# One tap of the first half of the channels of a depthwise convolution: 64-row matmuls in two of four residues replaced by an addition on VectorE, with the residues and the parts of an iteration in another order

## The chip, the cores and the metric

The kernel runs on 1 core of one Trainium2 chip. The metric is the device time of one launch in microseconds (us). Before the change it is 1837.94 us, the median of 3 runs (1837.26 to 1841.47).

## What is computed

Input x has the shape (4, 128, 96, 96). It is normalised by groups of channels, and then a small state-space layer runs over the image four times: along rows, along rows backwards, along columns, along columns backwards. The four results are mixed by a 1x1 convolution (`fuse_w`) and added to x. One direction is:

```
t = grouped1x1(x, in_proj_w)               # 512 channels: 256 of u, 256 of gate
u = conv5(silu(u))                         # depthwise, 5 taps along the sequence
s = ssm_in(u);  a = 0.999 + 0.0009 * sigmoid(ssm_delta(u))
b, c = tanh(ssm_b(u)), tanh(ssm_c(u))
h = scan(h * a + b * s)                    # written with cumulated logarithms
u = u + ssm_out(c * h + d * s)
y = out_proj(mix(u * sigmoid(gate)))
```

All is float32. The first 128 channels of u and the other 128 take different ways in the kernel, called j = 0 and j = 1 below.

## The kernel before, in words

**Units.** A batch has two phases, order V (columns) and H (rows), and each of them works on the forward and the backward direction at once, called s = 0 and s = 1. A phase has NS = 6 steps of 16 lines. Positions of a line are taken modulo R = 4, and one iteration `t` does one such *residue* p of one step: 384 positions (N) of both directions. So there are 4 x 2 x 6 x 4 = 192 iterations; `k = t % 4` is the place in the step, and in the kernel before k is also p. In the second half of a phase the two directions meet the lines that the other one has had, so that the activations `sil` and the gates are not computed again but read back, mirrored, from copies in DRAM (`kept`, `kept_sil`; `fresh(step)` and `mirror(n)` say which).

**The convolution.** Five taps. For j = 1 the taps are ScalarE's first (L718) and four multiply-adds on VectorE (L720, the last one into `u`), in PSUM banks 0 and 1. For j = 0 `sil` keeps the four residues in the four groups of 32 partitions, so that one matmul sums over residues: `conv` has 8 matmuls of 128 rows by 32 columns (weights `band`) over one of two neighbouring columns, and the rest of the taps lie in the other column: `less_both` has 8 matmuls of 64 rows by 32 columns (weights `less`). `less_rows` picks the 64 rows. For residues 1 and 2 two of the residues in those rows have a tap; for residues 0 and 3 only one tap lies there, so that half of these 64 rows meet weights of zero. PSUM is then copied to `u` by L1063. The trace has two records, called passes here, for each matmul in the program.

**One iteration** (`pair_of_tiles`, t >= 8; `pair` does the first eight). It works on the convolution of iteration t, and on the gating and output of iteration n = t - 6 (LAG), whose units are `bi` and `bi + 1`. In TensorE's order the parts are called as follows.

- *W*: `accumulate`, twice 8 matmuls of 128 rows with `w_fin` for iteration n - 1. ScalarE copies the product to `ys` (L825, L827), and GpSimd adds it to `acc` (L844).
- *conv* and *less*: as above, into banks `cb`.
- *block*: 32 matmuls of 32 by 32, in which four row groups work at a time: 16 tiles of input projection (`in_proj_tile`, for the step ahead) or gate (`gate_tile`), called `tile_x` after the change, and 16 tiles of `out_tile` (ssm_out of bi), which add to banks 0 to 3. Two loops, j = 1 and j = 0. Input and gate tiles go to banks `cb` and `db`.
- *proj*: 16 matmuls of 128 rows of iteration t (`w_proj`, operand `main` in the profile), into `db`. ScalarE makes `tm` (L757), copies half of `tb` (L758) and takes the tanh of the other half (L763); GpSimd makes the decay and the product (L765, L766).

Around it: `under(bi, s)` (L553) copies u of n into banks 2s and 2s + 1, so that out_tile adds to it. Bank 0 and 1 are also those of the taps: `under(bi, 0)` can only follow the last tap of iteration t, and the next first tap only the gating of bi. `gating` (L659) is VectorE's, two an iteration. `scale_s` (L775) is a ScalarE multiply. The activations of the block are silu (L491, L500) or tanh (L557, L563). `scan` (L792) runs in k < 2 for the step before; `outputs` (L798 to L801) is GpSimd's. `stats_chunks` (L405) takes statistics of the next batch, `stats_finish` hands out its end in small pieces at k > 1.

**Order of the work.** It is written by hand: the code's order is each engine's order. All loads and stores (`load_front` L280, `load_gate` L295, `load_chunks` L401, `load_kept` L598 and L600, `keep_silu` L468, `load_silu` L475, `send` L807, the reload L1018, the kept gates L1095) are issued by SyncE (SP in the profile), in order, each one waiting for what it needs before the next can leave.

Of the kernel before, what the change touches and what calls it, by code (L numbers as in the profile page):

```python
# [47 lines left out]
P = 128  # L48
# [8 lines left out]
R = 4  # L57
# [5 lines left out]
UB = 8  # L63
NP = NS * R


@with_exitstack
def conv_preact_kernel(
# [28 lines left out]
    for ph, (b, order, dirs) in enumerate(phases):  # L97
        for st in range(NS):
            for p in range(R):
                for s in range(2):  # L100
                    units.append(
                        {
                            "b": b,
                            "order": order,
                            "lay": dirs[s][0],
                            "dir": dirs[s][1],
                            "st": st,
                            "step": ph * NS + st,
                            "p": p,
                            "s": s,  # L110
                            "k": 2 * p + s,
                            "id": f"{ph}_{st}_{p}_{s}",
                        }
                    )
# [172 lines left out]
    def mirror(n):  # L287

        return None if n % NP < NP // 2 else NP - 1 - n % NP

# [42 lines left out]
    b_in, w_tap, b_proj = w_small[:, 64:72], w_small[:, 72:77], w_small[:, 77:79]  # L333
    d_sb, b_mix, b_out, b_fuse = (w_small[:, a:b] for a, b in ((79, 80), (80, 82), (82, 83), (83, 84)))
    w_out = w_out_fuse[:, 0:HID]
    w_fuse = w_out_fuse[:, HID : HID + 4 * P].rearrange("p (d c) -> p d c", d=4)
# [18 lines left out]
    id32 = wp.tile([P, 32], F32, name="id32")  # L355
    ident = wp.tile([P, P], F32, name="ident")
    make_identity(nc, ident)
# [3 lines left out]
    for s in range(2):  # L361
# [21 lines left out]
    kept = [  # L383
        [dp.tile([P, 2, 2, N], F32, tag=f"kept{e}_{m}", name=f"kept{e}_{m}") for m in range(NP // 2 - 2)]
        for e in range(2)
# [4 lines left out]
    def chunks_of(t):  # L390

        un = units[2 * t]
        b, k = un["b"] + 1, t % R
        if un["order"] == "V" and b < B and k > 1:
            return [(b, un["st"] * R + 2 * (k - 2) + e) for e in range(2)]
        return []

    def load_chunks(t):
        for b, c in chunks_of(t):
            chunks[b, c] = wk.tile([P, SC], F32, tag="xs", bufs=4, name=f"xs_{b}_{c}")  # L400
            nc.sync.dma_start(chunks[b, c], xr[b, :, bass.ts(c, SC)])  # L401
# [169 lines left out]
    def sigmoids(bi, to):  # L571
        bn = stats[units[bi]["b"]][1]
        n = bi // 2
        gv = gates[n % 2]
        for s in range(2):

            for j in (1, 0) if s and to == GATE[False] else (0, 1):
                nc.scalar.activation(
                    gv[:, s, j, :],
                    bank(to[2 * s + j])[:, :N],  # L580
                    AF.Tanh,
                    bias=bn[:, 2 + j : 3 + j],
                    scale=0.5,
                )
            load_gate(bi + s + UB)
        if n % NP < NP // 2 - 2:
            nc.sync.dma_start(kept[n // NP % 2][n % NP], gv)

    old_gates = {}

    def tile_of(n):
        m = mirror(n)
        return gates[((n % NP if m is None else m) + n // NP) % 2]

    def load_kept(n):
        m = mirror(n)
        if n % NP < 3 and NP <= n < NU // 2:
            nc.sync.dma_start(tile_of(n), kept[n // NP % 2][n % NP])  # L598
        if n < NU // 2 - R and m is not None and m < NP // 2 - 2:
            nc.sync.dma_start(tile_of(n), kept[n // NP % 2][m])  # L600
# [70 lines left out]

    def conv(i, banks):

        step, p = units[i]["step"], units[i]["p"]
        sil, k, b0 = blocks(step), less_of(p), min(banks)
        for s in range(2):
            for g in range(4):
                mm(bank(b0 + s), g, band[:, s, p, g, :], columns(step, sil[s][:, g, :], 1 - k),
                   True, False)

# [131 lines left out]
    def accumulate(bu, bk, adder=nc.gpsimd, last=False):  # L812
# [9 lines left out]
        if not direct:  # L822
            ys = wk.tile([P, N], F32, tag="ys", bufs=4, name=f"ys_{bu['id']}")
            if s == 0 and bu["order"] == "H":
                nc.scalar.activation(ys, y, AF.Identity, bias=b_fin)  # L825
            else:
                nc.scalar.copy(ys, y)  # L827
            y = ys
# [11 lines left out]
        def add():  # L840
            if direct and s == 0:
                adder.scalar_tensor_tensor(part, y, b_fin, part, ALU.add, ALU.add)
            else:
                adder.tensor_add(part, y, part)  # L844
            if bu["order"] == "H" and bu["st"] >= NS // 2 and bu["p"] == R - 1:

                done.extend((b, bass.ts(2 * st + e, LN * WW // 2)) for e in range(2))
# [147 lines left out]
    def pair_of_tiles(t):  # L995
        i, k, n, end = 2 * t, t % R, t - LAG, NU // 2
        bi, last = 2 * n, t == end - 1
        cb, db = ((4, 5), (6, 7))[:: 1 if t % 2 == 0 else -1]
        late = (n - 1) % (NP * 2) == 0
        step, g = divmod(t + R, R)  # L1000
        fronted, gated = fresh(step), None
# [9 lines left out]
        for e in soon:  # L1011
            load_kept(e)
        soon.clear()
        if t < end - 2:
            send()
        if len(reload) == 4 and (k == 1 or late):
            for b, r in reload:
                nc.sync.dma_start(accf[:, r], xr[b, :, r])  # L1018
            reload.clear()
        if t == LAG + 2:  # L1020
            for j in (1, 0):
# [6 lines left out]
            for s in range(2):  # L1028
                load_gate(bi + s + UB)
        new_u(i)  # L1030
        taps(i, (1, 2))
        piece = later and k > 1
        if piece:
            free[0] = SSM + 2
            next(later[0], None)
        taps(i, (3, 4))
        if piece:
            next(later[0], None)
# [9 lines left out]
        held.clear()  # L1048
        adds = [accumulate(waiting.pop(0), b, *((nc.vector, True) if last else ())) for b in db]
        if late:  # L1050
            held.extend(adds)
        else:
            for add in adds:
                add()

        conv(i, cb)
        under(bi, 0)
        less_both(i, cb)
        if k == 1:
            outputs(i - 10)  # L1060
        stats_chunks(t)
        for s, copy in enumerate((nc.scalar.copy, nc.scalar.copy if k < 2 else nc.vector.tensor_copy)):
            copy(us[i][:, s, 0, :], bank(cb[s])[:, :N])  # L1063
# [12 lines left out]

        if fronted:
            for s in range(2):
                silu(step, g, s, 1, db[s])
        elif gated is not None:  # L1080
            for s in range(2):
                tanh_one(gated, to, s, 1, db[s])
        gating(bi, 0)
        first_tap(i + 2)
# [7 lines left out]
        elif gated is not None:  # L1092
            tanh_both(gated, to, 0, cb[0])
            if gated % NP < NP // 2 - 2:
                nc.sync.dma_start(kept[gated // NP % 2][gated % NP], to)  # L1095
# [5 lines left out]
        un = units[i]  # L1101
        if un["order"] == "V" and un["b"] + 1 < B and un["st"] == NS - 1 and k == R - 1:
# [20 lines left out]
    def tail():  # L1123
# [66 lines left out]
        for i, s, e in ((-2, 1, 0), (-1, 0, 0), (-1, 0, 1), (-2, 1, 1), (-1, 1, 0), (-1, 1, 1)):  # L1190
# [17 lines left out]
            else:  # L1208
                nc.vector.scalar_tensor_tensor(part, y, b_fin, part, ALU.add, ALU.add)
            if bu["p"] == R - 1:  # L1210
                region = bass.ds(lines * WW, LN // 2 * WW)
                nc.sync.dma_start(out[bu["b"], :, region], accf[:, region])

    def start():
# [42 lines left out]
        def burst(j, g):  # L1257
            for s in range(2):
                in_proj(0, g, s, j, banks[j][g][s])

        def silus(j, g):
            for s in range(2):
                silu(0, g, s, j, banks[j][g][s])
            edges(0, g, j, nc.vector)
# [7 lines left out]
        silus(0, 0)  # L1272
        burst(1, 0)
        silus(0, 1)
        burst(1, 1)
        silus(0, 2)
# [5 lines left out]
        load_rows(0, slice(0, R))  # L1282
        load_rows(1, slice(0, 1))
        silus(0, 3)
        new_u(0)
        burst(1, 2)
        silus(1, 0)
        taps(0, (0,), nc.vector)
        burst(1, 3)
        load_rows(1, slice(1, R))  # L1290
        silus(1, 1)
        taps(0, (1,))
        conv(0, head_banks(0))
        silus(1, 2)
        taps(0, (2,))
        silus(1, 3)
        conv_less(0, head_banks(0))
# [101 lines left out]
```

## Time and profile before

| | |
|---|---|
| median of 3 runs | 1837.94 us |
| the profiled execution | 1845.45 us |
| its span in the trace | 1843.6 us |
| granted TensorE clock (full is 1) | 0.998 |
| DMA | 338.55 MB, mean 184 GB/s, main queue 58.8% of 16 engines |
| DMA issues by SyncE of sil to DRAM and back | 128 of 770.0 KB |
| xs (statistics) loads | 72 of 192.0 KB |

How to read the lines below: in a timeline, the start, the duration, the engine, the line of the kernel, the operation, the operands and the count; in brackets how long the engine sat idle before it and what ended that. In a list of groups, the busy time and the mean of one in ns stand behind the first bar and the idle time ahead of the group behind the second. In a list of windows, busy time and count stand for PE, PEld, DVE, ACT and POOL, and then the clock, the DMA share and GB/s. PE is TensorE, PEld its weight loads, DVE is VectorE, ACT ScalarE, POOL GpSimd. A busy TensorE can still hold a wait between overlapping passes.

### The profile page before, as it was taken

The numbers are of one execution on the slowest core, as the hardware profiler recorded it, in microseconds if no ns is written. First come the engines' busy times: TensorE is split into PE (matmuls) and PEld (weight loads), VectorE is DVE, ScalarE is ACT, GpSimd is POOL, SyncE is SP. The second block draws the span as 40 slices with busy tenths as digits, with TensorE's granted clock in tenths as the row PEclk, the third lists the DMA queues.
The fourth block names the chain that finished last, engine by engine and source line by source line (L and its number), as shares of the span: only waits on it lengthen the run. The fifth ranks groups of instructions, "written<-read, shape, count | busy, mean of one in ns | idle before, by whom it ended". The sixth has DMA issues, their size and how long they took to land.

```text
span 1843.6 us, 70463 instructions
## 1 busy us (share of the span) xinstructions
PE 1815.0 (98%) x30762; PEld 679.5 (37%) x30762; DVE 1462.7 (79%) x1526; ACT 1537.8 (83%) x2607; POOL 1478.9 (80%) x1477
## 2 busy tenths in 40 slices
PE   7999999999999999999999999999999999999998
PEld 3333333333333333333333333333333333333343
DVE  6878887887778888777777888878777777777787
ACT  4888888888888888888888888888888888888875
POOL 3578888888778888887877888888788888887886
PEclk9999999999999999999999999999999999999999
DMA  8655674446965577345796558633578545754424
GB/s 240 178 185 169 192 205 128 159 143 184 305 229 186 171 213 191 113 153 155 221 289 220 168 179 220 185 120 135 177 226 276 196 142 167 192 153 151 148 100 177
DMA packets 151124, 338.55 MB, mean 184 GB/s; under 512 B 14496, under 2 KB 116256, under 8 KB 150816
## 3 DMA queue, kind: packets, MB, share of 16 engines
q1 hardware_dynamic: 150672, 334.00, 58.8%
q8 instruction: 243, 3.98, 0.9%
q14 instruction: 65, 0.53, 0.1%
q10 hardware_dynamic: 144, 0.04, 0.0%
HBM read 201.73 MB, written 132.25 MB: 181 GB/s over the span
## 4 chain that ended last, share of the span: by engine, by line
PE 96%; DVE 1%; DMA 1%; ACT 1%; issue 1%; SPq 0%; DVEq 0%
PE psum L134 95%; DMA xs<-in_xr 1%; DVE psum L720 0%; DMA acc<-in_xr 0%; PE psum L1216 0%; PE psum L541 0%; DVE u L659 0%; DVE t L792 0%; DVE u L720 0%; PE psum L521 0%; ACT psum L718 0%; SPq L307 0%; ACT psum L553 0%; PE psum L1223 0%; PE psum L1231 0%
## 5 line engine op out<-in xcount | busy, mean ns | idle before, releaser
L720 DVE SCALAR_TENSOR_TENSOR psum<-sil,small,psum 128x768 f32<-128x768 f32 x576 | 589.0, 1023 | 27.8 <-ACT psum L718 3.8
L134 PE MATMUL psum<-u,main 128*32 128x384 f32 x6144 | 538.8, 490 | 5.1 <-DVE u L720 2.6
L134 PE MATMUL psum<-u,w_fin 128*32 128x384 f32 (+1 forms) x6192 | 535.7, 485 | 5.4 <-ACT gate L563 3.2
L844 POOL TENSOR_TENSOR acc<-ys,acc 128x384 f32<-128x384 f32 x375 | 451.3, 1226 | 74.1 <-ACT ys L825 32.4
L659 DVE SCALAR_TENSOR_TENSOR u<-gate,psum 128x768 f32<-128x768 f32 x376 | 349.8, 952 | 157.6 <-PE psum L134 88.4
L134 PE MATMUL psum<-x_in,wn 32*32 32x385 f32 (+1 forms) x6080 | 361.5, 493 | 0.0
L134 PE MATMUL psum<-t,main 32*32 32x384 f32 x5888 | 351.0, 492 | 0.3 <-ACT psum L553 0.2
L765 POOL TENSOR_SCALAR t<-tm 64x384 f32<-64x384 f32 x191 | 177.6, 930 | 181.5 <-ACT tm L757 156.6
L553 ACT COPY psum<-u 128x768 f32<-128x768 f32 x380 | 308.0, 811 | 9.8 <-DVE u L659 3.8
L134 PEld LDWEIGHTS psum<-u,w_fin 128*32 128x32 f32 x6192 | 202.4, 110 | 297.2 <-issue 245.0
L134 PEld LDWEIGHTS psum<-u,main 128*32 128x32 f32 x6144 | 183.2, 110 | 346.6 <-issue 209.3
L799 POOL TENSOR_TENSOR t<-t,t 64x384 f32<-64x384 f32 (+1 forms) x192 | 295.2, 1537 | 15.1
L134 PE MATMUL psum<-sil,band 128*32 128x384 f32 x3072 | 285.2, 485 | 0.0
L798 POOL TENSOR_TENSOR t<-t,t 64x384 f32<-64x384 f32 (+1 forms) x192 | 234.4, 1221 | 20.7 <-DVE t L792 4.5
L766 POOL TENSOR_TENSOR t<-t,tm 64x384 f32<-64x384 f32 x192 | 199.0, 1036 | 16.4 <-ACT t L758 1.2
L1063 ACT COPY u<-psum 128x384 f32<-128x384 f32 x276 | 123.2, 481 | 97.9 <-PE psum L134 97.9
L134 PEld LDWEIGHTS psum<-x_in,wn 32*32 32x32 f32 x6080 | 123.8, 103 | 212.1 <-ACT psum L553 108.8
L718 ACT ACTIVATE psum<-sil,small 128x768 f32<-128x768 f32 x191 | 173.2, 907 | 33.2 <-DVE u L659 12.7
L720 DVE SCALAR_TENSOR_TENSOR u<-sil,small,psum 128x768 f32<-128x768 f32 x192 | 194.9, 1015 | 6.9
L1063 DVE COPY u<-psum 128x384 f32<-128x384 f32 x92 | 51.3, 558 | 155.0 <-PE psum L134 154.1
L134 PE MATMUL psum<-sil,less 64*32 64x384 f32 x3072 | 168.1, 495 | 0.0
L134 PEld LDWEIGHTS psum<-sil,band 128*32 128x32 f32 x3072 | 101.4, 110 | 148.4 <-issue 76.5
(109 smaller groups left out, 1597.3 us busy)
## 6 DMA issues: line engine op xcount, KB each, us to landing
sil<-sil SPq DMA_DIRECT2D x128, 770.0 KB, 6.6
gate<-kept SPq DMA_DIRECT2D x97, 768.0 KB, 6.9
kept<-gate SPq DMA_DIRECT2D x59, 768.0 KB, 3.6
x_in<-in_xs SPq DMA_DIRECT2D x192, 96.2 KB, 3.6
out<-acc SPq DMA_DIRECT2D x48, 384.0 KB, 6.1
kept<-shared SPq DMA_DIRECT2D x21, 768.0 KB, 3.6
acc<-in_xr SPq DMA_DIRECT2D x39, 384.0 KB, 7.4
xs<-in_xr SPq DMA_DIRECT2D x72, 192.0 KB, 6.1
```

The costliest lines, as they stand in the source:

```text
L134: nc.tensor.matmul(o[r, : rhs.shape[-1]], lhsT, rhs, start=start, stop=stop, skip_group_check=True)
L553: nc.scalar.copy(psum[:, ssm(bi, s) : ssm(bi, s) + 2, :N], us[bi][:, s])
L659: nc.vector.scalar_tensor_tensor(v, g, 1.0, pz, ALU.add, ALU.mult)
L718: nc.scalar.activation(part, src, AF.Copy, scale=w_tap[:, 0:1])
L720: nc.vector.scalar_tensor_tensor(us[i][:, :, 1, :] if k == K - 1 else part, src, w_tap[:, k : k + 1], part, ALU.mult, ALU.add,)
L765: nc.gpsimd.tensor_scalar(*decay(i))
L766: nc.gpsimd.tensor_mul(ta[0:64, p, :], tb[0:64, :], tm[0:64, :])
L798: engine.tensor_mul(ta[0:64, p, r], tb[64:P, r], ta[64:P, p, r])
L799: engine.tensor_add(tb[0:64, r], ta[0:64, p, r], tb[0:64, r])
L844: adder.tensor_add(part, y, part)
L1063: copy(us[i][:, s, 0, :], bank(cb[s])[:, :N])
```

## The change

1. The residues of a step are done in the order `TURN = (1, 2, 3, 0)`, so k no longer equals p. `mirror` follows, and the second half of a phase no longer meets the gates in strictly reversed order: all 12 gates of a half phase are written to DRAM and read back (before: 10), and `tile_of(n)` is `gates[n % 2]`.
2. In residues 3 and 0 (`single`, k = 2 and 3), `less_both` is not done. `load_lone` copies the one residue that the missing tap needs, from `sil` to a tile `lone` that has the channel order of `u`: 16 DMAs of 32 x 384 values per step, at k = 0, from `blocks(step)`, which holds the j = 0 half. `add_lone` multiplies by the tap's weight, adds what conv left in PSUM and writes `u`, on VectorE; there is no copy to `u` then. In the other two residues ScalarE makes one copy of 128 x 768 to `u`.
3. The parts of an iteration stand in another order: conv, less, copy or add, W, block, proj. `cb` is always banks 6 and 7 and `db` 4 and 5.
4. The block has another order of tiles, `under(bi, 0)` another place, and the first gating is written between the two one-bank activations.
5. `ys` and `xs` have 3 buffers instead of 4; the statistics loads are spread otherwise over a phase. The first eight iterations keep their less matmuls.

```diff
-        cb, db = ((4, 5), (6, 7))[:: 1 if t % 2 == 0 else -1]
+        cb, db = (6, 7), (4, 5)
+        un = units[i]
+        single = alone(un["p"])
...
+        if k == 0 or t == LAG + 2:
+            load_lone(un["step"])
...
+        new_u(i)
+        conv(i, cb, single)
+        taps(i, (1, 2))
+        piece = later and k > 1
...
+        taps(i, (3, 4))
...
         under(bi, 1)
         if t > LAG + 2:
             scale_s(i - 4)
+        if single:
+            add_lone(i, cb)
+        else:
+            less_both(i, cb)
+            nc.scalar.copy(us[i][:, :, 0, :], psum[:, cb[0] : cb[0] + 2, :N])
+        if not single:
+            under(bi, 0)
         if k < 2:
             scan(t // R - 1, k)
...
-        adds = [accumulate(waiting.pop(0), b, *((nc.vector, True) if last else ())) for b in db]
+        adds = []
+        for s in range(2):
+            adds.append(accumulate(waiting.pop(0), db[s], *((nc.vector, True) if last else ())))
+            if s == 0 and single:
+                under(bi, 0)
...
-        conv(i, cb)
-        under(bi, 0)
-        less_both(i, cb)
...
-        for s, copy in enumerate((nc.scalar.copy, nc.scalar.copy if k < 2 else nc.vector.tensor_copy)):
-            copy(us[i][:, s, 0, :], bank(cb[s])[:, :N])
...
-        for j in (1, 0):
-            for c in range(4):
-                for s in range(2):
-                    if fronted:
-                        in_proj_tile(step, g, s, j, (cb, db)[j][s], c)
-                    elif gated is not None:
-                        gate_tile(gated, s, j, (cb, db)[j][s], c)
-                for e in range(2):
-                    out_tile(bi, 1 - j, e, c)
...
+        def tile_x(s, j, c):
+            e = s if fronted else 1 - s
+            bk = db[s] if j else cb[e]
...
+        for c in range(4):
+            tile_x(0, 1, c)
+            out_tile(bi, 0, 0, c)
+            out_tile(bi, 0, 1, c)
+            out_tile(bi, 1, 1, c)
+        for c in range(4):
+            out_tile(bi, 1, 0, c)
+            tile_x(0, 0, c)
+            tile_x(1, 0, c)
+            tile_x(1, 1, c)
...
+    def load_lone(step):
+        for p in (R - 1, 0):
+            lone[p] = wk.tile([P, 2, N], F32, tag="lone", bufs=2, name=f"lone{p}_{step}")
+            e = less_of(p) if fresh(step) else 1 - less_of(p)
+            for s in range(2):
+                q = R - 1 - p if s else p
+                for g in range(4):
+                    nc.sync.dma_start(
+                        lone[p][32 * g : 32 * g + 32, s, :],
+                        blocks(step)[s][32 * q : 32 * q + 32, g, e : e + N],
+                    )
+
+    def add_lone(i, banks):
+        step, p = units[i]["step"], units[i]["p"]
+        src = lone[p] if fresh(step) else lone[p][:, :, ::-1]
+        nc.vector.scalar_tensor_tensor(
+            us[i][:, :, 0, :],
+            src,
+            w_edge[:, less_of(p) ^ 1 : (less_of(p) ^ 1) + 1],
+            psum[:, banks[0] : banks[0] + 2, :N],
+            ALU.mult,
+            ALU.add,
+        )
```

More of the change, by code (lines that the diff above doesn't have):

```diff
@@ L64 @@
 NP = NS * R
+TURN = (1, 2, 3, 0)
 @with_exitstack
@@ L383, in conv_preact_kernel @@
     kept = [
-        [dp.tile([P, 2, 2, N], F32, tag=f"kept{e}_{m}", name=f"kept{e}_{m}") for m in range(NP // 2 - 2)]
+        [dp.tile([P, 2, 2, N], F32, tag=f"kept{e}_{m}", name=f"kept{e}_{m}") for m in range(NP // 2)]
         for e in range(2)
@@ L393, in chunks_of @@
         b, k = un["b"] + 1, t % R
-        if un["order"] == "V" and b < B and k > 1:
-            return [(b, un["st"] * R + 2 * (k - 2) + e) for e in range(2)]
+        if un["order"] == "V" and b < B:
+            m = t % NP
+            first = m - 2 + (m > 8) + (m > 16)
+            return [(b, first + e) for e in range(1 + (m in (8, 16)))] if m > 1 else []
         return []
@@ L670, in blocks, with conv @@
         return [sils[step][:, s if fresh(step) else 1 - s, 0] for s in range(2)]
-    def conv(i, banks):
+    def conv(i, banks, alone=False):
         step, p = units[i]["step"], units[i]["p"]
```

93 lines of the change are left out of this document (49 added, 44 removed).

## The prediction, made before the changed kernel ran

> **What bounds the kernel now.** I read the page first: busy shares, then the chain that ended last.
>
> ```profile
> PE 1815.0 (98%) x30762; PEld 679.5 (37%) x30762; DVE 1462.7 (79%) x1526; ACT 1537.8 (83%) x2607; POOL 1478.9 (80%) x1477
> ...
> PE 96%; DVE 1%; DMA 1%; ACT 1%; issue 1%; SPq 0%; DVEq 0%
> ```
>
> TensorE is busy for 98% and is 96% of the chain, so a matmul taken away shortens the run as long as nothing else is late. But the other three engines stand at 79 to 83%, and they are tied to TensorE by one shared pair of PSUM banks. So I looked for the steady period, from the start of the first tap (L718) at t = 8 and at t = 184, the last with input tiles in its block.
>
> ```profile
> 101.88 0.91 ACT L718 ACTIVATE psum<-sil,small 128x768 f32<-128x768 f32 x1
> 1750.21 0.91 ACT L718 ACTIVATE psum<-sil,small 128x768 f32<-128x768 f32 x1
> ```
>
> That is 176 iterations in 1648.33 us, 9.37 each. One iteration, from the timeline:
>
> ```profile
> 604.64 1.01 DVE L405 BATCH_NORM_STATS2 bn<-xs 128x6 f32<-128x384 f32 x2
> ...
> 606.70 0.51 PE L134 MATMUL psum<-x_in,wn 32*32 32x384 f32 x2
> ...
> 606.97 0.56 DVE L1063 COPY u<-psum 128x384 f32<-128x384 f32 x1 [1.31 <-PE psum L134]
> ...
> 607.39 0.70 PE L134 MATMUL psum<-x_in,wn 32*32 32x384 f32 x2
> 607.59 0.51 PE L134 MATMUL psum<-t,main 32*32 32x384 f32 x2
> ...
> 607.76 1.05 ACT L557 ACTIVATE gate<-psum,bnorm 128x384 f32<-128x384 f32 x2 [0.43 <-PE psum L134]
> ...
> 607.94 1.82 DVE L659 SCALAR_TENSOR_TENSOR u<-gate,psum 128x768 f32<-128x768 f32 x2 [0.42 <-PE psum L134]
> ...
> 608.17 0.50 PE L134 MATMUL psum<-t,main 32*32 32x384 f32 x2
> ...
> 608.60 2.79 PE L134 MATMUL psum<-u,main 128*32 128x384 f32 x32
> 608.93 0.91 ACT L718 ACTIVATE psum<-sil,small 128x768 f32<-128x768 f32 x1
> ...
> 609.78 0.88 ACT L563 ACTIVATE gate<-psum,bnorm 128x768 f32<-128x768 f32 x1
> 609.87 3.14 DVE L720 SCALAR_TENSOR_TENSOR psum<-sil,small,psum 128x768 f32<-128x768 f32 x3
> ...
> 610.56 0.57 ACT L757 ACTIVATE tm<-psum,small 128x384 f32<-128x384 f32 x1
> ...
> 611.21 2.76 PE L134 MATMUL psum<-u,w_fin 128*32 128x384 f32 x32
> ...
> 611.46 0.47 ACT L758 COPY t<-psum 64x384 f32<-64x384 f32 x1 [0.33 <-PE psum L134]
> ...
> 613.05 1.01 DVE L720 SCALAR_TENSOR_TENSOR u<-sil,small,psum 128x768 f32<-128x768 f32 x1
> ...
> 613.79 1.47 PE L134 MATMUL psum<-sil,band 128*32 128x384 f32 x16
> ...
> 614.02 0.86 ACT L827 COPY ys<-psum 128x384 f32<-128x384 f32 x2
> ...
> 614.77 0.82 ACT L553 COPY psum<-u 128x768 f32<-128x768 f32 x1
> 615.19 0.88 PE L134 MATMUL psum<-sil,less 64*32 64x384 f32 x16
> ...
> 616.00 0.51 PE L134 MATMUL psum<-x_in,wn 32*32 32x384 f32 x2
> ```
>
> The starts of TensorE's groups give their true lengths: block 606.70 to 608.60 = 1.90, proj 2.61, W (w_fin) 2.58, band 1.40, less 0.81: sum 9.30, with no gap between groups. A few longer iterations make the rest of 9.37; I leave them as they are. Inside the block there is a hidden wait: its second loop starts with 607.39, but the next tile starts only at 607.59, 0.06 after VectorE's copy of u (606.97 + 0.56 = 607.53) has freed the bank. That 0.20 counts as busy time.
>
> **The change part by part.** Residues 0 and 3 ("single" iterations) do without the 64-row matmuls: 92 of them from t = 8, 88 among the 176.
>
> (1) TensorE, less matmuls gone:
>
> ```profile
> L134 PE MATMUL psum<-sil,less 64*32 64x384 f32 x3072 | 168.1, 495 | 0.0
> L693 ACT COPY u<-psum 128x768 f32<-128x768 f32 x3 | 2.4, 798 | 1.6 <-PE psum L134 1.6
> ```
>
> 3072 recorded passes are 16 in each of 192 iterations, 0.88 us busy each; by starts 0.81 (615.19 to 616.00). I use 0.81: 88 x 0.81 = 71 us gained.
>
> (2) The wait inside the block goes. The conv now comes ahead of W, so u is copied (or added by VectorE) before the block opens and the banks of its second loop are free. Gain 0.20 in every iteration: 176 x 0.20 = 35 us. The block is then 1.70; not less, because proj's first half needs the first tanh (607.76 + 0.53 = 1.59 after the block's start) and comes close behind it.
>
> (3) One more change of tile height in the other iterations ("double"): order band 128 rows, less 64, W 128, block 32. Band to less costs 0.10 now (band 1.40 where half of W's 2.58 is 1.29); I take 0.10 for W to block and less to W is in less's 0.81. So 88 x 0.10 = 9 us lost. Single iterations go 128 to 32 rows at 0.10, in band's place. The Trainium skill, "TensorEngine Tiling (Array Packing)", section Key Properties, says that a change of tiling mode drains TensorE, which speaks against moving the conv. The trace agrees: after the last block pass at 608.17 (0.50 long) proj starts at 608.60, 0.43 on, where a wave of W follows the last after 0.32 (2.58 over eight waves of four). Counting by that rule: three changes per iteration before, four in double and two in single ones after, so the sum by it would be about zero in place of minus 9.
>
> TensorE alone then needs 1.70 + 2.61 + 1.30 + 2.58 + 0.10 = **8.29** in single and 1.70 + 2.61 + 1.40 + 0.81 + 2.58 + 0.10 = **9.20** in double iterations.
>
> (4) What comes late next: ScalarE's order. The block cannot open before under(bi, 0) has refilled banks 0 and 1, nor before the first ys copy has freed its bank. I follow ScalarE from the block's start. In the block's new tile order the second tanh's tiles are the last ones, so it starts after the block: last pass at 1.70 - 0.43 = 1.27, plus 0.50, plus 0.08: 1.85 (before: both tanh ended at 2.11). Then first tap 2.40 (before 2.23), 0.85 to the double tanh 3.25, 0.78 to tm 4.03, 0.57 to the copy of tb 4.60 (proj's result is there at 1.70 + 2.61 + 0.25 = 4.56). From that copy to the end of scale_s it is 611.46 to 614.02 = 2.56: 7.16.
> Single: first ys copy at 7.16 (W's first half ends 7.15), 0.43 to under(bi, 0) at 7.59; VectorE's taps end at 2.40 + 0.94 + 4.19 = 7.53, in time; + 0.82 = 8.41, + 0.06: block at 8.47, and 8.57 where ys adds the bias. Against 8.29 TensorE waits 0.18 to 0.28.
> Double: copy of u (0.80, L693), under(bi, 0) 0.82, ys 0.43 to 0.53, 0.06: block at 9.27 to 9.37 against 9.20.
> I take 8.52 and 9.32, mean 8.92, against 9.30: 0.38 x 176 = **67 us gained**.
>
> (5) VectorE. The added operation has the form of a tap, 1.02. It replaces 92 copies of 0.56. Single: gating 1.82, taps 4.19, the add 1.02, at most 1.01 of statistics: 8.04 of 8.52. Double: 1.82 + 4.19 + a scan of 2.10 (row below) = 8.1 of 9.32. The add runs from 7.53 to 8.55, and proj needs its u at 8.52 + 1.70. It waits for nothing late; behind it are statistics and the next gating at 8.52 + 1.24. So nothing, as long as the add's data is there. Small pieces of the next batch's statistics run between taps at k > 1, which are now the single iterations without slack.
>
> ```profile
> L792 DVE TENSOR_TENSOR_SCAN t<-t,t 64x768 f32<-64x768 f32 x40 | 84.0, 2100 | 1.3
> L190 DVE BATCH_NORM_AGGREGATE mv<-bn 128x2 f32<-128x144 f32 x4 | 3.2, 799 | 0.0
> L201 DVE SCALAR_TENSOR_TENSOR ex<-dev,mv 128x1 f32<-128x1 f32 x4 | 4.0, 1009 | 0.1
> ```
>
> About 3 us in each of three batches, 0 to 9 us lost; I take 5.
>
> (6) GpSimd keeps its instructions; 641 busy of 770 in a steady stretch (row below), 7.7 per iteration, under 8.52.
>
> (7) SyncE: 46 steps x 16 copies of 48 KB (`lone`), behind gate loads, and all gates kept and reloaded (2 of 12 more per phase each way, 16 of each).
>
> ```profile
> 980.00:1750.00 770.00, 770.00 (x13284) 284.88 (x13276) 608.61 (x613) 659.80 (x1116) 640.61 (x621) 1.00 0.58 179
> ```
>
> ```profile
> 610.68 0.33 SPq L1095 DMA_DIRECT2D kept<-gate  x1
> ```
>
> ```profile
> 1109.25 2.27 SPq L295 DMA_DIRECT2D x_in<-in_xs  x2
> ```
>
> ```profile
> gate<-kept SPq DMA_DIRECT2D x97, 768.0 KB, 6.9
> ...
> x_in<-in_xs SPq DMA_DIRECT2D x178, 48.1 KB, 3.5
> ```
>
> One issue takes 0.33 to 1.14 us, so 16 take 5 to 18 us of a step's 35.7. They start at the end of iteration k = 3 and are used two iterations later, so they are in time. The DMA share is 0.58, and some 63 MB on 338 MB make it about 0.7. I take nothing, and say below where that ends.
>
> Sum: 67 - 5 = 62 us, from the median 1837.94 (the profiled execution took 1845.45, 7.5 more; the steps are differences, so I apply them to the median): **1776 us**. The first eight iterations and the last seven I leave unchanged.
>
> **Rivals.**
> (a) *ScalarE's order eats more.* If the block stays at 1.90 (its tiles now write other banks and the wait returns elsewhere), every time in (4) moves by 0.20: 8.72 and 9.52, mean 9.12, gain 0.18 x 176 = 32, less 5: 1811 us. For it: single iterations have no slack on three engines at once. Against: the copies that caused the 0.20 are out of the block.
> (b) *TensorE never waits.* Mean 8.745, gain 0.555 x 176 = 98: 1740 us. For it: ScalarE's rows overlap by 0.03 to 0.1 each, and my chain may be long by that.
> (c) *The copies for `lone` block SyncE, slower than before.* It decides through the gate load queued behind them: the k = 3 iteration frees SyncE at about 3.4, the 16 copies run to 3.4 + 16c, the next gate load lands 6.9 later, and must be there for the gating that comes 8.52 + 2 x 9.32 + 1.24 = 28.4 after the same start. That holds up to c = 1.13 us per copy, and beyond it each step pays 16 (c - 1.13). At c = 1.22 the 62 us are gone; at c = 1.5 each of 46 steps pays 5.9, 272 us: 2048 us. For it: the x_in pair at 1.14 each stands right at the point. Against: other issues take 0.33 to 0.5, and the x_in rows are of 64 partitions, these of 32. The Trainium skill, "DMA: Bandwidth & Descriptors", section Bandwidth, calls transfers under 64 KB dominated by descriptors; the trace agrees in that 48 KB land in 3.5 us; its 0.95 us for 64 KB would by itself, as an estimate, give 15 us for 16 and no stall.
> (d) *No change in time*: (a) and a small part of (c) together. That the change does not do what it says I exclude: 736 of 1536 less matmuls and all copies of u inside the block are gone from the program.
>
> **How the numbers follow.** Forecast (1745 to 1803) 0.62; (a) 0.14; (b) 0.07; (d) 0.05; (c) 0.12. The range runs from just under (b), 1738, to just over (a), 1815, and leaves out (c), (d) and the tails. Faster by over 0.3% (5.5 us, about what a measurement of this kernel tells from no change): 0.83; within: 0.05; slower: 0.12.
>
> **What would show it.** Right: first-tap periods that alternate two near 9.3 and two near 8.5; a block of 1.7; small TensorE gaps ahead of the block released by L560 (under) in single and by the ys copy in double iterations. Wrong: gaps at gating or at the lone add released by a DMA, periods of a step that are long at k = 1 or 2, or GpSimd's ys additions (bufs 3) that hold ScalarE.

## The result, and the profile after

The changed kernel takes **1956.27 us** (median of 4 runs, 1942.3 to 1960.2); the kernel before, run beside it again, 1839.7 (1837.26 to 1842.79). The ratio is 1.0619 [1.0562, 1.0676]: slower by 6.2%, where I forecast 3.4% faster. The profiled execution took 1960.2 us, its span is 1958.5, its granted clock 0.968.

Page of the changed kernel: busy times, and the chain that ended last by engine and by line.

```profile
PE 1817.6 (93%) x29290; PEld 692.4 (35%) x29290; DVE 1490.0 (76%) x1526; ACT 1499.8 (77%) x2423; POOL 1439.4 (73%) x1477
...
PE 73%; DMA 14%; DVE 4%; ACT 4%; SPq 3%; POOL 2%; issue 1%; DVEq 0%; ACTq 0%; POOLq 0%
PE psum L135 73%; DMA gate<-kept 5%; DMA kept<-shared 3%; DVE psum L754 2%; DMA acc<-in_xr 2%; DMA x_in<-in_xs 1%; ACT psum L752 1%; DMA lone<-sil 1%; SPq L281 1%; DVE u L664 1%; DMA xs<-in_xr 1%; POOL acc L878 1%; DMA out<-acc 1%; ACT psum L560 0%; DVE u L754 0%
```

TensorE's part of the chain falls from 96 to 73%; DMAs rise from 1 to 14%. That is a kernel that mostly runs as planned and now and then stands still for a transfer. First taps (L752) in a quiet stretch, from ScalarE's timeline:

```profile
595.22 0.90 ACT L752 ACTIVATE psum<-sil,small 128x768 f32<-128x768 f32 x1
603.86 0.90 ACT L752 ACTIVATE psum<-sil,small 128x768 f32<-128x768 f32 x1
612.50 0.90 ACT L752 ACTIVATE psum<-sil,small 128x768 f32<-128x768 f32 x1
621.94 0.90 ACT L752 ACTIVATE psum<-sil,small 128x768 f32<-128x768 f32 x1
```

Two periods of 8.64, then one of 9.44 (two in a step, 9.43 elsewhere): the alternation that the prediction asked for. Over 176 iterations the mean of 9.035 against 9.32 before is 0.285 x 176 = 50 us gained. Now ScalarE's timeline where it goes wrong, at iterations 16 to 19 of a phase of 24 (here and below iterations are counted within their phase):

```profile
185.28 0.90 ACT L752 ACTIVATE psum<-sil,small 128x768 f32<-128x768 f32 x1
186.11 0.89 ACT L570 ACTIVATE shared<-psum,bnorm 128x768 f32<-128x768 f32 x1
...
204.75 1.05 ACT L564 ACTIVATE shared<-psum,bnorm 128x384 f32<-128x384 f32 x2 [12.80 <-DMA kept<-shared]
205.69 0.91 ACT L752 ACTIVATE psum<-sil,small 128x768 f32<-128x768 f32 x1
...
216.93 0.90 ACT L752 ACTIVATE psum<-sil,small 128x768 f32<-128x768 f32 x1
```

This period is 20.41 and the next 11.24. In iterations 17 to 19 the gates go through `shared`, a tile of one buffer: the tanh of one iteration fills it, SyncE writes it to DRAM as `kept`, and only then may the tanh of the next one begin. The tanh ended at 186.11 + 0.89 = 187.00. SyncE's timeline shows when the write left:

```profile
168.15 0.33 SPq L1148 DMA_DIRECT2D kept<-gate  x1
...
174.20 14.91 SPq L698 DMA_DIRECT2D lone<-sil  x16
189.21 0.53 SPq L1148 DMA_DIRECT2D kept<-gate  x1
...
192.36 0.38 SPq L605 DMA_DIRECT2D gate<-kept  x1
192.78 1.25 SPq L482 DMA_DIRECT2D sil<-sil  x2
...
196.27 0.54 SPq L1148 DMA_DIRECT2D kept<-shared  x1
...
222.07 11.85 SPq L698 DMA_DIRECT2D lone<-sil  x16
```

The 16 copies hold SyncE from 174.20 to 189.11; the queue behind them (a kept gate, a gate load and two of sil at 768 to 770 KB each, between them x_in and xs) follows in a bunch, and the write of `shared` leaves at 196.27, 9.3 us after its data were there (6.3 to 9.3 at the seven turns). It then shares the DMA engines with the bunch and lands 8 us later. The first row is the write of iteration 15's gate, which the kernel before does not make; it waited 5.3 us for its own tanh, and the copies stand behind it. In the kernel before the same pair stood like this, the write 0.03 us behind the tanh:

```profile
186.58 0.88 ACT L563 ACTIVATE shared<-psum,bnorm 128x768 f32<-128x768 f32 x1
...
187.49 0.34 SPq L1095 DMA_DIRECT2D kept<-shared  x1
```

The waits of the changed kernel (total us, times, longest) tell how often:

```profile
ACT shared L564 <- DMA kept<-shared: 79.2, 7, 12.8
...
DVE u L664 <- DMA gate<-kept: 47.5, 16, 5.7
```

Seven times, once in each phase but one. The sum over iterations 9 to 184 closes the account. I take each period minus its steady value (8.64 or 9.43) and add: 171 us too long, 90 of them at iterations 18 and 19. Before, the same sum is 1648.33 - 176 x 9.32 = 8. So 171 - 8 - 50 = 113 us lost, and 117 were measured.

### The profile page after: what moved, and what is told of

The parts are those of the page before. It is cut to its first block, busy times and chain, and to the rows that moved or that the text cites. A ratio compares the mean times of both kernels' runs of the same rounds, so it can differ in the third digit from the quotient of the medians.

```text
span 1958.5 us, 68596 instructions
## 1 busy us (share of the span) xinstructions
PE 1817.6 (93%) x29290; PEld 692.4 (35%) x29290; DVE 1490.0 (76%) x1526; ACT 1499.8 (77%) x2423; POOL 1439.4 (73%) x1477
## 2 busy tenths in 40 slices
DMA packets 191088, 399.81 MB, mean 204 GB/s; under 512 B 26816, under 2 KB 152128, under 8 KB 190784
## 4 chain that ended last, share of the span: by engine, by line
PE 73%; DMA 14%; DVE 4%; ACT 4%; SPq 3%; POOL 2%; issue 1%; DVEq 0%; ACTq 0%; POOLq 0%
PE psum L135 73%; DMA gate<-kept 5%; DMA kept<-shared 3%; DVE psum L754 2%; DMA acc<-in_xr 2%; DMA x_in<-in_xs 1%; ACT psum L752 1%; DMA lone<-sil 1%; SPq L281 1%; DVE u L664 1%; DMA xs<-in_xr 1%; POOL acc L878 1%; DMA out<-acc 1%; ACT psum L560 0%; DVE u L754 0%
## 5 line engine op out<-in xcount | busy, mean ns | idle before, releaser
L135 PE MATMUL psum<-u,main 128*32 128x384 f32 x6144 | 557.0, 504 | 79.0 <-ACT shared L564 73.1
L878 POOL TENSOR_TENSOR acc<-ys,acc 128x384 f32<-128x384 f32 x375 | 410.1, 1115 | 133.1 <-ACT ys L859 61.4
L135 PE MATMUL psum<-x_in,wn 32*32 32x385 f32 (+1 forms) x6080 | 397.6, 499 | 10.9 <-DMA x_in<-in_xs 4.1
L135 PE MATMUL psum<-t,main 32*32 32x384 f32 x5888 | 340.1, 492 | 2.7 <-ACT psum L560 2.6
L135 PE MATMUL psum<-sil,band 128*32 128x384 f32 x3072 | 292.5, 494 | 26.2 <-ACT sil L507 24.5
L135 PEld LDWEIGHTS psum<-u,w_fin 128*32 128x32 f32 x6192 | 191.7, 110 | 322.1 <-issue 227.5
L752 ACT ACTIVATE psum<-sil,small 128x768 f32<-128x768 f32 x191 | 172.0, 901 | 38.9 <-DVE u L664 38.1
L135 PEld LDWEIGHTS psum<-x_in,wn 32*32 32x32 f32 x6080 | 140.7, 103 | 160.3 <-ACT ys L861 63.9
L498 ACT ACTIVATE sil<-psum,bnorm 128x385 f32<-128x385 f32 x216 | 122.3, 582 | 97.4 <-PE psum L135 95.8
L861 ACT COPY ys<-psum 128x384 f32<-128x384 f32 x281 | 134.5, 479 | 51.0 <-PE psum L135 39.3
L135 PEld LDWEIGHTS psum<-t,main 32*32 32x32 f32 x5888 | 118.0, 103 | 61.1 <-issue 41.1
```

The lines of the kernel that those rows point to most:

```text
L135: nc.tensor.matmul(o[r, : rhs.shape[-1]], lhsT, rhs, start=start, stop=stop, skip_group_check=True)
L498: nc.scalar.activation(sils[step][:, s, j, g, :], bank(bk)[:, : N + 1], AF.Silu, bias=bn[:, 1:2] if j else bn[:, 4 + g : 5 + g],)
L752: nc.scalar.activation(part, src, AF.Copy, scale=w_tap[:, 0:1])
```

## The experiments

Theory **N**: the 16 small copies of a step hold SyncE by their number, and what stands behind them comes too late. Rivals: **B**, their bytes overload the DMA engines; **R**, the new order itself (residues, conv ahead of W, all gates kept) is the slow part; later **X** and **W**, below. The expectations of e1 to e4 call N by the letter S and R by the letter O. Each table entry is the median in us, the ratio to the kernel before in the same batch, the sum of long periods as above, and its part at iterations 18 and 19 of a phase.

```
kernel             median   ratio [95%]              long    at 18, 19
after              1956.27  1.0619 [1.0562, 1.0676]  171.0   90.4
e1_no_copies       1818.01  0.9898 [0.9881, 0.9914]   37.3    4.9
e2_less_back       1887.5   1.0284 [1.0258, 1.0309]   27.5    0.2
e3_before_copies   1862.67  1.0149 [1.0134, 1.0164]   33.4    7.2
e4_spread          1913.49  1.0427 [1.0411, 1.0442]  130.9   57.2
e5_bounce          1857.06  1.0127 [1.0103, 1.0151]   73.2   40.3
e6_bounce_ys4      1933.35  1.0533 [1.0514, 1.0552]  148.4   37.8
e7_tiny            1914.46  1.0436 [1.0419, 1.0454]  128.6   84.1
e8_before_gates    1941.65  1.0582 [1.0562, 1.0602]  111.3   92.3
e9_best            1815.88  0.9884 [0.9859, 0.9910]   30.2    3.2
e10_early          1930.63  1.0520 [1.0483, 1.0558]  146.5   91.3
e11_skew           1812.95  0.9871 [0.9841, 0.9902]   29.0    2.6
```

### e1: the change without its copies

```diff
-        if k == 0 or t == LAG + 2:
-            load_lone(un["step"])
...
-        src = lone[p] if fresh(step) else lone[p][:, :, ::-1]
+        sil = sils[step][:, :, 1] if fresh(step) else sils[step][:, ::-1, 1, ::-1]
+        src = columns(step, sil[:, :, 0, :], 0)
```

> The changed kernel without load_lone: the 736 copies of 48 KB are left out, and add_lone reads a piece of sil of the same shape in their place (so u holds wrong values in residues 0 and 3; every other instruction stays). Theory S (the 16 copies in a row hold SyncE 12 to 15 us at k = 0, and the kept write of the one-buffer tile shared and the gate loads behind them leave late): the 171 us of long periods vanish, the periods stay 9.43 and 8.64, and the time is 1838 - 176 x 0.28 = 1788 us, 1780 to 1800. Rival O (the new order of parts and tiles, or the mirrored order with all 12 gates through DRAM, makes the long periods): about 1940 to 1955 us, as the changed kernel.

1818.01, between the two expectations and 18 above the first: the copies cost 138 us, and all else together gains 1%. The periods stay 9.43 and 8.64, so the steady gain of 50 us does not hang on them. R falls as the main cause. 37 us of long periods remain. Some of those are at the end of a batch, where `ys`, now asked for earlier against GpSimd's additions, waits for a third buffer; from ScalarE's timeline:

```profile
539.75 0.48 ACT L862 COPY ys<-psum 128x384 f32<-128x384 f32 x1 [3.45 <-POOL acc L879]
```

### e2: the new order with the less matmuls everywhere, no copies

```diff
-        single = alone(un["p"])
+        single = False
...
-        if k == 0 or t == LAG + 2:
-            load_lone(un["step"])
```

> The changed kernel with the less matmuls in all residues, no copies and no add: what is left is the new order of residues and parts and the 12 kept gates. Theory S: no long periods, every iteration is a double one of 9.43, so 1838 + 176 x 0.11 = 1857 us, 1848 to 1867. Rival O: the long periods stay, 1950 to 2030 us.

1887.5, and the steady period is 9.43 to 9.44 in every residue. With less an iteration is 0.11 slower than before (9.32), without it 0.80 faster than that. I expected 1857 and missed by 30: 0.11 x 176 = 19 and 20 more of long periods than before explain 39 of the 52 us on 1835.3. The other 13 are a matter of which executions were profiled: these took 1881.48 here and 1845.45 in the kernel before, 36 apart. So the order is a cost of its own, and all that the change gains comes from the 88 iterations without less.

### e3: the copies alone, in the kernel before

```diff
+        if k == 0 or t == LAG + 2:
+            copies(units[i]["step"])
```

`copies` makes the same 16 transfers into tiles that nobody reads. (To make room for them `ident` is laid into another tile, as in the changed kernel.)

> The kernel before with the same 16 copies per step added at the same place (k = 0, ahead of the sends), into a tile that nothing reads; the result is not touched. Theory S: the same long periods at the shared tile and the gate loads, somewhat shorter since SyncE has 37.3 us per step in place of 36.1 and two gates less per half phase: 1838 + 80 to 170 = 1918 to 2008 us. Rival O: 1838 to 1848 us, since neither order nor gates have changed.

Only +27 us, between the 80 or more of N and the 10 at most of R. The copies hold SyncE there just as long (13.27 us in the middle of 46 steps; 13.47 in the changed kernel). But at the turn they start 20 us before the tanh of iteration 17 ends, in place of 13, and fewer large transfers stand behind them. The write of `shared` is mostly in time (7.5 us of waits in all):

```profile
162.16 13.51 SPq L688 DMA_DIRECT2D lone<-sil  x16
...
178.08 1.25 SPq L475 DMA_DIRECT2D sil<-sil  x2
...
182.02 0.35 SPq L1109 DMA_DIRECT2D kept<-shared  x1
```

So N by itself is not enough. New theory **X**: the copies and the additional gate traffic (all gates of a phase kept and reloaded, four transfers more per phase, all at the turn) together. e8 tests it.

### e4: the same copies in two groups of eight, at the ends of k = 0 and k = 1

```diff
+        if k < 2 and t > LAG + 3:
+            load_lone(un["step"], ((R - 1, 0)[k],))
```

> The changed kernel with the same 16 copies per step, but 8 at the end of k = 0 (for residue 3) and 8 at the end of k = 1 (for residue 0), behind the kept writes and gate loads of their iteration. Theory S (a run of 16 in front of urgent transfers): 8 copies take 6 to 7.5 us of an iteration of 9.4, so the kept write of shared leaves in time and most of the 171 us goes: 1790 to 1835 us. Rival B (the added bytes or descriptors on the 16 DMA engines slow all transfers): unchanged, 1930 to 1960 us. Rival O: unchanged as well.

-43 us only, outside all three expectations. Each group holds SyncE about 6.6 us, and the second one now lies between two writes of `shared`, so that 57 of 90 us stay at iterations 18 and 19.

### e5: fewer, larger transfers with twice the bytes

```diff
+                nc.sync.dma_start(
+                    edge[step % 2][p // 3][:, s, :].rearrange("(g c) n -> c g n", g=4),
+                    blocks(step)[s][32 * q : 32 * q + 32, :, e : e + N],
+                )
...
+            nc.sync.dma_start(lone[p], edge[step % 2][p // 3])
```

Four writes of 192 KB to DRAM at the start of k = 0, two reads of 384 KB at its end: 6 issues in place of 16.

> The changed kernel with the 16 copies of a step replaced by 4 writes of 192 KB to DRAM at k = 0 and 2 reads of 384 KB at the end of k = 0: 6 issues instead of 16, twice the bytes. Theory N (what costs is the number of copies that SyncE issues one after the other, each holding a place in its queue): most of the 138 us that the copies cost goes, 1820 to 1855 us. Theory B (what costs is the bytes on the DMA engines): 1956 us or more.

1857.06: 99 us less than the changed kernel, although it moves more (435.91 MB against 399.81). SyncE's timeline:

```profile
167.85 2.65 SPq L701 DMA_DIRECT2D edge<-sil  x4
...
176.10 0.90 SPq L709 DMA_DIRECT2D lone<-edge  x2
```

3.6 us of SyncE in place of 14.9. The number of issues counts for more than the bytes: N against B. It is not the number of DMA packets either, which rises from 191088 to 195498. Against e1 the six transfers still cost 39 us, and 40 us are left at 18 and 19.

### e6: e5 with one buffer for the read and four for ys

```diff
-            lone[p] = wk.tile([P, 2, N], F32, tag="lone", bufs=2, name=f"lone{p}_{step}")
...
+        lone[p] = wk.tile([P, 2, N], F32, tag="lone", bufs=1, name=f"lone{p}_{step}")
...
-            ys = wk.tile([P, N], F32, tag="ys", bufs=3, name=f"ys_{bu['id']}")
+            ys = wk.tile([P, N], F32, tag="ys", bufs=4, name=f"ys_{bu['id']}")
...
+        if k in (0, 2):
+            load_lone(un["step"], R - 1 if k == 0 else 0)
```

> As e5_bounce, but one lone buffer (the read for residue 0 leaves at the end of k = 2), and with the room ys has 4 buffers again. Theory N: as e5_bounce, less the 10 us that ScalarE waits for a third ys buffer at the three batch ends (3.3 us each in e1_no_copies, and their echo): 1808 to 1845 us. Theory B: 1945 us or more.

1933.35, slower than e5 by 76 and 88 above the expected range, by an edit of mine: with one buffer the second read can start only late, and VectorE's add waits for it 35 times.

```profile
DVE u L713 <- DMA lone<-edge: 111.9, 35, 5.3
```

The other half worked: with four buffers the long period at iteration 8 (end of a batch) fell from 8.5 us in all to 0.5.

### e7: the sixteen copies at a twelfth of their bytes

```diff
-                        lone[p][32 * g : 32 * g + 32, s, :],
-                        blocks(step)[s][32 * q : 32 * q + 32, g, e : e + N],
+                        lone[p][32 * g : 32 * g + 32, s, 0:32],
+                        blocks(step)[s][32 * q : 32 * q + 32, g, e : e + 32],
```

> The changed kernel with all 736 copies, each of 32 x 32 values (4 KB) in place of 32 x 384 (48 KB), and add_lone reading a piece of sil of the same shape (wrong values in residues 0 and 3). Theory N: number and place of the issues are the same, so 1900 to 1956 us. Theory B: one twelfth of the bytes, so nearly e1_no_copies, 1818 to 1835 us.

1914.46: with 4 KB a copy 96 of the copies' 138 us remain, and 84 of the 90 at iterations 18 and 19. The rest, 42 us, is the price of the bytes. SyncE is held 12.04 us all the same (from 168.36). Windows (busy time of PE, PEld, DVE, ACT, POOL, then the clock, the DMA share, GB/s) show what that does, first two of e7, then two of the changed kernel, the copies and what follows them:

```profile
170.00:180.00 10.00, 10.00 (x176) 3.64 (x168) 8.78 (x9) 8.68 (x15) 6.89 (x7) 1.00 0.19 54
180.00:198.00 18.00, 7.84 (x132) 3.11 (x128) 6.88 (x8) 6.68 (x13) 8.70 (x9) 0.75 0.93 317
```

```profile
174.20:189.11 14.91, 14.91 (x261) 5.71 (x250) 13.38 (x15) 12.86 (x21) 11.51 (x12) 1.00 0.46 141
189.11:205.00 15.89, 4.29 (x92) 1.74 (x84) 4.56 (x6) 2.87 (x6) 6.44 (x7) 0.73 0.97 322
```

While SyncE works through the small copies of e7, the DMA engines are used to 0.19 in the window of 10 us (0.30 over all 12.04); then the large transfers come at once, at 0.93 and 317 GB/s, and TensorE is busy 7.84 of 18 us. In the changed kernel the shares are 0.46 and 0.97. Without copies (e1) the share is 0.90 from 165 to 180 us and 0.91 from 180 to 195, and the period at iteration 18 is 9.86 in place of 20.41. So the engines have little to spare at the turn, and what they do not move during the copies is left for the time behind them.

### e8: the kernel before with the copies and four more gate writes at the turn

```diff
+        if t % NP in (15, 16, 17):
+            for _ in range(2 if t % NP == 16 else 1):
+                nc.sync.dma_start(more, tile_of(n + 1 if t % NP < 17 else n))
```

> e3_before_copies with four more writes of 768 KB from the gate tiles to DRAM per phase, at the end of iterations 15, 16 (two) and 17 of a phase, which is as much as the changed kernel's two more gates written and read back at that place. Theory X (the copies alone have room in the old iteration, and cost so much only together with the added gate transfers at the turn of a phase, just ahead of the one-buffer tile shared): the long periods at iteration 18 of a phase grow from 6 us to 40 to 90 in all, 1900 to 1955 us. Rival (the shorter single iterations or the new order make the difference): 1862 to 1875 us.

1941.65, 79 us more than e3, and 92.3 us at iterations 18 and 19: a stall like that of the changed kernel, in the old one. The first line is from the waits, the others from SyncE's timeline:

```profile
ACT shared L559 <- DMA kept<-shared: 84.0, 7, 13.5
...
168.64 12.36 SPq L690 DMA_DIRECT2D lone<-sil  x16
...
191.75 0.44 SPq L1111 DMA_DIRECT2D kept<-shared  x1
```

X holds in kind: copies alone +27, both together +107. But the four writes do more than move bytes. SyncE works in order, and the one at iteration 15 waits for its gate (6.9 us at this turn; 5.3 for the same write in the changed kernel), so that the copies start 13.5 us before the tanh of iteration 17 ends, where e3 had 19.8 and the changed kernel has 12.8. Besides, all four go to one tile in DRAM, and SyncE waited for one to land before it issued the next (24.6 us in all, 2.8 at this turn), which the changed kernel does not do. How much of the 79 us each of these makes is not shown.

### e10: the fifth step's copies one iteration earlier

```diff
-        if k == 0 or t == LAG + 2:
+        if k == 0 and un["st"] != 4:
             load_lone(un["step"])
...
+        if k == R - 1 and un["st"] == 3:
+            load_lone(un["step"] + 1)
```

> The changed kernel with the 16 copies of the fifth step of each phase issued at the end of iteration 15 of the phase in place of the start of iteration 16 (their source is there since iteration 11); nothing else moves. Theory X (SyncE's queue is full just where the tile shared has to be handed on): the 90 us of long periods at iterations 18 and 19 fall under 25, the rest stays, 1875 to 1905 us. Rival (the copies cost the same wherever they stand): 1940 to 1960 us.

1930.63 lies outside both expectations, and the 90 us at 18 and 19 did not go (91.3). The copies were out of the way, but the sil loads that had been issued ahead of them now came behind them, and so later:

```profile
165.16 11.45 SPq L698 DMA_DIRECT2D lone<-sil  x16
...
176.71 1.26 SPq L482 DMA_DIRECT2D sil<-sil  x2
...
189.15 0.34 SPq L1148 DMA_DIRECT2D kept<-shared  x1
```

ScalarE's timeline:

```profile
180.20 0.89 ACT L570 ACTIVATE shared<-psum,bnorm 128x768 f32<-128x768 f32 x1
198.16 1.05 ACT L564 ACTIVATE shared<-psum,bnorm 128x384 f32<-128x384 f32 x2 [12.11 <-DMA kept<-shared]
```

The write left 8.1 us after its tanh, in place of 9.3, and took 8.7 us more to land, in place of 8, since now the engines were full. The window from first tap to first tap (columns as in e7), share 1.01:

```profile
179.38:199.10 19.72, 8.43 (x144) 3.50 (x140) 7.91 (x9) 7.26 (x13) 10.06 (x10) 0.83 1.01 347
```

So the wait has two parts: the write leaves late behind the bunch, and it lands among it. Moving the copies alone exchanges one for the other.

### e9: e5 with room at the turn

```diff
-        elif st == NS - 1 and g < 2:
-            load_silu(step, (2 * g, 2 * g + 1))
+        elif st == NS - 1:
+            load_silu(step, (g,))
...
-            ys = wk.tile([P, N], F32, tag="ys", bufs=3, name=f"ys_{bu['id']}")
+            ys = wk.tile([P, N], F32, tag="ys", bufs=4, name=f"ys_{bu['id']}")
...
+        elif k == 1 and un["st"] == 3:
+            save_lone(un["step"] + 1)
...
+        elif k == R - 1 and un["st"] == 3:
+            load_lone(un["step"] + 1)
```

Six transfers a step, those of the fifth step ahead of the turn, the four sil loads one an iteration, four buffers for ys (and one for tm, to make room).

> e5_bounce (4 writes and 2 reads per step) with the fifth step's writes and reads moved to iterations 13 and 15, the four loads of sil for the sixth step spread over iterations 16 to 19, four ys buffers and one tm buffer. Theory X: of e5_bounce's 73 us of long periods the 40 at iterations 18 and 19 and the 8.5 at the batch ends go, 1805 to 1825 us, faster than the kernel before. Rival: 1840 to 1860 us.

1815.88, 0.9884 [0.9859, 0.9910]: 1.2% faster than the kernel before, and within the noise of e1, which has no copies at all, but three buffers for ys. At 18 and 19 there are 3.2 us left, and 5.4 at iteration 20. How much each of its edits gives was not run apart. SyncE's timeline at the turn, one sil load an iteration:

```profile
179.03 1.46 SPq L482 DMA_DIRECT2D sil<-sil  x1
...
185.06 0.34 SPq L1158 DMA_DIRECT2D kept<-shared  x1
```

### e11: is the 0.20 in the block a wait for a bank?

The block still takes 1.90 (next section), though no copy of u is pending. Theory **W**: the second loop's x tiles wait for the ys copy of W's second half. The edit moves them one place later, on e9:

```diff
-            tile_x(1, 1, c)
+            if c:
+                tile_x(1, 1, c - 1)
+        tile_x(1, 1, 3)
```

> e9_best with the tiles of the block that wait for the second ys copy one place later in the second loop (the last one alone at the end). Theory W (the block stays at 1.90 us because these tiles wait for that copy, in the place of the copy of u before): the block falls by 0.1 to 0.2 us in 176 iterations less 0.08 for the lone tile, 0 to 20 us faster than e9_best. Rival (the block is 1.9 us long by itself): 5 to 15 us slower than e9_best.

The steady periods stay 9.44 and 8.64, and 1812.95 against 1815.88 lies within both intervals. The ys copy and the weight loads at the boundary:

```profile
584.53 0.48 ACT L869 COPY ys<-psum 128x384 f32<-128x384 f32 x1 [0.33 <-PE psum L135]
...
585.07 0.10 PEld L135 LDWEIGHTS psum<-t,main 32*32 32x32 f32 x1 [0.22 <-issue]
585.26 0.13 PEld L135 LDWEIGHTS psum<-x_in,wn 32*32 32x32 f32 x3
```

The ys copy ended at 585.01, ahead of both rows, and the pause of 0.19 is between them, ahead of a tile that no longer waits for that copy. W falls too.

## Why the prediction was wrong

One double and one single iteration of the changed kernel, from the timeline, carry points 1 to 4:

```profile
590.01 2.79 PE L135 MATMUL psum<-u,w_fin 128*32 128x384 f32 x32
592.73 0.51 PE L135 MATMUL psum<-x_in,wn 32*32 32x384 f32 x1
...
594.63 2.79 PE L135 MATMUL psum<-u,main 128*32 128x384 f32 x32
...
600.26 1.01 DVE L706 SCALAR_TENSOR_TENSOR u<-lone,small,psum 128x768 f32<-128x768 f32 x1
600.44 0.81 ACT L560 COPY psum<-u 128x768 f32<-128x768 f32 x1
601.22 0.51 PE L135 MATMUL psum<-x_in,wn 32*32 32x384 f32 x1
601.40 0.52 PE L135 MATMUL psum<-t,main 32*32 32x384 f32 x3
```

- **(1) Less gone: right.** 0.81 forecast; 9.44 with less everywhere (e2) against 8.64 without is 0.80.
- **(2) The block's wait goes: wrong, 35 us.** 592.73 to 594.63 is 1.90, as before, not 1.70. I read a copy that ended 0.06 ahead of the next tile as its cause. The pause of 0.19 is there with the copy long done, at the boundary between the block's two loops. What makes it stays open; e11 excludes the ys copy.
- **(3) One more change of tile height: right in size.** 0.10 forecast for W in front of the block; W takes 590.01 to 592.73 = 2.72 in place of 2.58, so 0.14.
- **(4) ScalarE's order: right for single iterations, not for double ones.** Forecast 8.52 and 9.32, measured 8.64 (8.74 where ys adds its bias) and 9.43. The block in a single iteration opens 0.03 before under(bi, 0) ends at 601.25, and its next tile starts only at 601.40, so that it takes 2.05: it waits for ScalarE as worked out, 0.15 where 0.18 to 0.28 was forecast, but from a block of 1.90. In the double iteration the groups follow each other without such a wait (2.60 + 1.40 + 0.81 + 2.72 + 1.91 = 9.44): with a block of 1.90 TensorE is the later one. The times are nearly those of rival (a).
- **(5) VectorE: right in size.** The add is 1.01. In three batches the periods at iterations 6, 14 and 15 are 9.26, 9.30 and 9.24, where pieces of the statistics run: about 6 us.
- **(6) GpSimd: right in steady work, incomplete at the end of a batch** (ys, e1 and e6), a few us.
- **(7) SyncE, "I take nothing": the step that failed.** Rival (c) had the mechanism, and I gave it 0.12 with a point of decision: no loss up to 1.13 us per copy. The copies took 14.91 / 16 = 0.93 and 11.85 / 16 = 0.74 (0.98 at most over all steps), *below* that point, and the loss came: 163 us more of long periods, where the sum had 5. I worked the point out for one consumer, the gate load two iterations later, which has 28 us. At the turn a consumer stands in the same queue that has none: the write of `shared`, whose tile has one buffer and whose next tanh comes one iteration on. I named the kept and reloaded gates in (7) and then priced the copies alone; e1, e3 and e8 show that only both together make the large stall (-17, +27 and +107 us). The gate loads that I did look at wait as well (47.5 us), behind the same queue.

Mean DMA share misled me too: 0.58 going to 0.7 looked like room. At the turn it is 0.46 during the copies and 0.97 behind them.

Open: how e8's 79 us divide, how SyncE's 0.74 to 0.93 us per copy divides into issuing and waiting for a place in the queue, what makes the 0.19 in the block, and most of some 30 us of long periods in the new order that neither copies nor the turn explain (e2, e9).

## What to carry to other kernels

Before adding transfers to a queue written in order, list everything that stands behind them until the next iteration, and find the one with the least slack: here a tile of one buffer that is handed on through DRAM; the slack of the other consumers says nothing about it. Price small transfers by their number on the issuing engine, and try fewer, larger ones even at twice the bytes (99 us here). Look at the DMA share in windows around the tightest hand-over, not at its mean, and take nothing for hidden because it is hidden in most iterations.

## What the runs showed of the hardware

A copy of 4 KB holds SyncE nearly as long as one of 48 KB: 12.04 us for sixteen at the turn (e7) against 14.91, and 12.22 against 13.47 in the middle of all 46 steps. In the changed kernel SyncE's own waits at these copies are for transfers that were issued before (total us, times, longest):

```profile
SPq L698 <- DMA sil<-sil: 45.8, 32, 3.2
SPq L698 <- DMA gate<-kept: 32.4, 19, 2.7
```

TensorE pays for a stop twice. The window of the changed kernel from the first tap after the stop to the next one, and the first proj after the stop:

```profile
205.69:216.93 11.24, 11.24 (x152) 4.06 (x148) 6.87 (x8) 7.49 (x13) 6.41 (x7) 0.80 0.84 276
```

```profile
205.38 5.10 PE L135 MATMUL psum<-u,main 128*32 128x384 f32 x32 [11.98 <-ACT shared L564]
```

After 11.98 us without work proj takes 5.10 in place of 2.79, at a granted clock of 0.54, and the iteration, with TensorE busy all the time at a granted clock of 0.80, takes 11.24 in place of 8.64: of these 2.6 us the clock makes, as an estimate, 0.20 x 11.24 = 2.2. The Trainium skill, "TensorE: Matmul & The Clock Gate", Part 1, says that after an idle window of about 3.4 us the clock falls to half until a busy window has passed; the trace agrees in kind, 2.79 / 5.10 being 0.55.
